# Attention computed for two batches in a row: TensorE's order in a fused graph layer with attention

## The chip, the cores and the metric

One core of a Trainium2 chip runs the whole kernel. The metric is the device time of one execution in microseconds (us), as the median of several executions. A single profiled execution gives the span that the views below are read from; in these runs it is 1.7 to 1.9 us shorter than the time.

Kernels are compared only within the same rounds. Ratios are computed as the mean time of one kernel's runs over that of the other's of the same rounds, so a ratio is not quite the ratio of the medians that I quote.

## The reference

Two layers over 128 batches of 128 nodes with 512 features, all in float32. Cut to what matters:

```python
# layer 0: conv with the adjacency matrix, maximum over features, residual, layer norm
A = einsum('od,bdn->bon', adj, x);  C = A + b          # W1 = W2 = adj
pre = A[:, :, None, :] + (C - A)[:, :, :, None]
x = layernorm(x + max(relu(pre), axis=-1))

# layer 1: masked attention with 8 heads of 64, projection, layer norm, residual, layer norm
q, k, v = split(x @ w_qkv)                              # 512 -> 3 * 512
attn = softmax(where(adj == 0, -inf, q @ k.T * 64 ** -0.5))
o = (attn @ v) @ w_proj + b_proj
x = layernorm(x + o + (layernorm(o) * gamma + beta))
```

## The kernel before

The 128 batches go through in 32 groups of four. TensorE does, per group, twelve products of 512 x 512 (eight for q and k over all four batches, four for v), four projections, and for every batch a convolution (`pa`), the transposes of x (`ptx`) and of the attention weights e (`ppt`), the scores (`psc`) and attention times v (`pav`).

Each product is done with split operands: an operand is cut into a high part and a low part, and a third form d corrects for what is lost. So a projection can start only when the output of attention has been split, which takes VectorE three operations and ScalarE one:

```python
def split(key, src, dsts):
    fh, fl, fd = dsts
    xh = work.tile([P, KC, P], FP, tag="xh", name=f"xh_{key}")
    nc.vector.tensor_scalar(xh.bitcast(I32), src.bitcast(I32), HIGH, None, op0=ALU.bitwise_and)
    hs[key] = fh, xh                                     # ScalarE casts xh into fh: split_high
    nc.vector.tensor_tensor(fl, src, xh, op=ALU.subtract)
    nc.vector.scalar_tensor_tensor(fd, fl.bitcast(FP), -HALF, xh, op0=ALU.mult, op1=ALU.add)

def product(key, two, terms):                            # terms: (stationary, moving) of h, l, d
    ...
    for kc in range(KC):
        h, l, _ = terms(kc)
        nc.tensor.matmul(pm, *h, start=(kc == 0), stop=False)
        nc.tensor.matmul(pm, *l, start=False, stop=(kc == KC - 1))
    for kc in range(KC):
        nc.tensor.matmul(pd, *terms(kc)[2], start=(kc == 0), stop=(kc == KC - 1))
```

The scores use 64 rows of the array, attention times v uses 64 columns, and everything else uses the full 128 x 128 (the trace writes the three as `64*128`, `128*64` and `128*128`):

```python
def scores(b):
    ...
        for s in range(2):
            hs = slice(s * HD, (s + 1) * HD)             # HD = 64
            nc.tensor.matmul(psc[:, s, hp, :], qkT[hs, hp, i, :], qkT[hs, KC + hp, i, :], ...)

def attend(b):
    ...
            nc.tensor.matmul(pavs[b][s * HD : (s + 1) * HD, hp, :],
                             v[:, h * HD : (h + 1) * HD], eT[:, s * HP + hp, :], ...)
```

The order is made by a plan. Every step is put down with a place in time, in planned microseconds; the list is sorted by place. On TensorE and ScalarE the sorted order is the order of the program; VectorE's order is chosen by a scheduler that takes the plan as its input. Before, the attention of a group is four blocks, one for each batch:

```python
for i in range(G):
    u = t + starts[i]
    last(0.0, transpose_e);  last(1.0, weights_T)        # batch of the group before
    now(0.95, scores);       now(2.1, masked);  now(3.5, row_max)
    nxt(2.0, transpose_x);   nxt(2.5, split_x)           # batch of the group after
    u += 2.5
    far(0.0, conv);          far(0.9, conv_max);  u += 0.9
    last(0.0, attend);       u += 1.0
    if i and 0 < g:
        projection((g - 1) * G + i - 1, u);  u += 2.8    # of the batch before
    last(0.1, heads)                                     # the split of attention's output
    ...                                                  # then a v product
```

## Time and profile before

| | before |
|---|---|
| time, median of 3 runs | 2081.63 us (2079.85 to 2081.64) |
| span of the profile | 2079.9 us |
| TensorE busy | 98% of the span |
| VectorE, ScalarE, GpSimd busy | 78%, 70%, 34% |
| first product of group 2 starts at | 144.02 us |
| from there to the first product of group 31 | 1837.96 us |
| from there to the end | 97.9 us |
| period of one group in the steady part | 63.467 us |

The lines are shown in the prediction. A line of a timeline gives the start, the duration, the engine, the source line, the operation, the tiles, the shapes and the count; matmuls overlap (in a product one is recorded as 0.40 us long and the next starts 0.23 us after it), so TensorE's time is read from start to start. A bracket at the end of a line is idle time of the engine before the instruction and what released it. "Period" in this document is always the time from the start of the first product of one group (the product (g, 4)) to that of the next.

### The profile page before, as it was taken

What the parts mean: (1) busy time and instruction counts of PE and PEld (TensorE: products, weight loads), DVE (VectorE), ACT (ScalarE), POOL (GpSimd) and SP (SyncE); (2) the same over time, 40 slices, a digit from 0 to 9 for tenths busy, and PEclk for the clock granted to TensorE, in tenths of its full rate; (3) what the DMA queues carried; (4) which work ended last, traced back from release to release, by engine and by line L of the source; (5) the groups of instructions that cost most, each with busy time, mean ns of one, the idle gap of its engine ahead of it and who ended that gap; (6) DMA issues with size and microseconds to landing.
All of it is one profiled execution on the core that took longest, in us unless ns stands there. A gap on an engine that the chain in (4) does not pass through costs nothing. (4 is left out here: it accounts for less than half of the span.)

```text
span 2079.9 us, 35025 instructions
## 1 busy us (share of the span) xinstructions
PE 2042.2 (98%) x12033; PEld 1591.0 (76%) x12033; DVE 1622.0 (78%) x2615; ACT 1451.7 (70%) x4130; POOL 701.5 (34%) x1329
## 2 busy tenths in 40 slices
PE   7899999999999999999999999999999999999997
PEld 5677777777777777777777777777777777777775
DVE  6787777887778877778877788777788777887787
ACT  5766767767767667677677676677776776766775
POOL 2123333323333233333233332333332333323434
PEclk8999999999999999999999999999999999999999
DMA  6345544455454455444554544554445545445533
GB/s 194 78 85 132 123 111 116 99 126 132 117 117 104 105 132 127 114 111 101 122 132 117 117 106 103 132 131 112 112 99 122 133 119 115 110 101 120 118 88 95
DMA packets 134434, 240.64 MB, mean 116 GB/s; under 512 B 14705, under 2 KB 18929, under 8 KB 134257
## 3 DMA queue, kind: packets, MB, share of 16 engines
q1 hardware_dynamic: 97680, 172.27, 27.1%
q0 software_dynamic: 36288, 66.08, 21.5%
q8 instruction: 95, 1.56, 0.3%
q14 instruction: 83, 0.67, 0.1%
q10 hardware_dynamic: 288, 0.07, 0.0%
HBM read 138.74 MB, written 100.66 MB: 115 GB/s over the span
## 5 line engine op out<-in xcount | busy, mean ns | idle before, releaser
L321 ACT ACTIVATE e<-e,nmax 128x128 f32<-128x128 f32 x1024 | 396.7, 391 | 6.3 <-DVE nmax L314 6.3
L380 POOL DMA_DIRECT2D xb<-o x124 | 120.2, 970 | 358.4 <-DVE o L385 342.1
L397 POOL TENSOR_SCALAR sum<-sum 128x1 f32<-128x1 f32 (+1 forms) x291 | 100.5, 345 | 391.5 <-ACT square L391 379.5
L213 POOL DMA_DIRECT2D x<-in_L_gnn_ln_beta_dram x128 | 115.6, 910 | 325.1 <-DMA x<-xt 308.3
L321 ACT ACTIVATION_READ_ACCUMULATOR e<-e,nmax 128x1 f32 x1024 | 194.1, 190 | 0.0
L398 POOL TENSOR_TENSOR sum<-sum,mhalf 128x1 f32<-128x1 f32 (+1 forms) x291 | 185.6, 638 | 22.5
L391 ACT ACTIVATE square<-o,sum 128x512 bf16<-128x512 f32 x256 | 183.2, 716 | 10.6 <-DVE o L385 8.7
L340 ACT COPY eT<-ppt 128x1024 f32<-128x1024 f32 x128 | 129.3, 1011 | 84.9 <-PE ppt L336 84.9
L349 PEld LDWEIGHTS pav<-eT,v 128*64 128x64 f32 x2048 | 109.2, 136 | 93.4 <-issue 47.4
L412 DVE SCALAR_TENSOR_TENSOR o<-o,sum,gamma_sb 128x512 f32<-128x512 f32 x128 | 96.1, 750 | 107.8 <-ACT square L391 104.8
L403 POOL TENSOR_SCALAR sum<-sum 128x1 f32<-128x1 f32 x256 | 157.5, 616 | 41.1 <-DVE o L385 35.6
L330 DVE TENSOR_TENSOR e<-e,sums 128x1024 f32<-128x1024 f32 x128 | 156.5, 1223 | 3.1
L306 DVE SCALAR_TENSOR_TENSOR e<-psc,mask 128x1024 f32<-128x1024 f32 x128 | 155.7, 1216 | 3.1 <-PE psc L299 3.0
L314 DVE TENSOR_REDUCE nmax<-e 128x8 f32<-128x1024 f32 x128 | 154.4, 1206 | 0.0
L299 PE MATMUL psc<-qkT 64*128 64x128 f32 x2048 | 149.9, 286 | 0.0
L299 PEld LDWEIGHTS psc<-qkT 64*128 64x128 f32 x2048 | 125.1, 188 | 24.1 <-issue 12.3
L349 PE MATMUL pav<-eT,v 128*64 128x128 f32 x2048 | 140.1, 279 | 2.1 <-ACT eT L340 2.1
L170 PE MATMUL pa<-xt,adjT 128*128 128x512 f32 x256 | 134.8, 612 | 2.7 <-DMA xt<-in_x_dram 2.3
L336 PE MATMUL ppt<-ident,e 128*128 128x128 f32 x1024 | 132.8, 273 | 0.0
L336 PEld LDWEIGHTS ppt<-ident,e 128*128 128x128 f32 x1024 | 119.5, 141 | 17.2 <-issue 0.5
L420 ACT ACTIVATE o<-o,sum 128x512 f32<-128x512 f32 x128 | 103.9, 811 | 33.5 <-POOL sum L406 33.4
L385 DVE SCALAR_TENSOR_TENSOR o<-o,sum,xb 128x512 f32<-128x512 f32 x128 | 95.7, 748 | 34.8 <-POOL sum L398 34.6
(4778 smaller groups left out, 5518.5 us busy)
## 6 DMA issues: line engine op xcount, KB each, us to landing
xt<-in_x_dram SPq DMA_DIRECT2D x128, 256.0 KB, 4.6
x<-xt SPq DMA_DIRECT2D x128, 256.0 KB, 3.3
x<-in_L_gnn_ln_beta_dram POOLq DMA_DIRECT2D x128, 256.0 KB, 6.4
xb<-x SPq DMA_DIRECT2D x128, 256.0 KB, 2.7
o<-in_L_gnn_b_proj_dram SPq DMA_DIRECT2D x128, 256.0 KB, 4.4
out_dram<-o SPq DMA_DIRECT2D x128, 256.0 KB, 2.3
xb<-o POOLq DMA_DIRECT2D x124, 256.0 KB, 3.5
wraw<-in_L_gnn_w_qkv_dram SPq DMA_DIRECT2D x12, 256.0 KB, 4.1
```

The costliest lines, as they stand in the source:

```text
L170: nc.tensor.matmul(pa[b], adjT, xs[b], start=True, stop=True)
L299: nc.tensor.matmul(psc[:, s, hp, :], qkT[hs, hp, i, :], qkT[hs, KC + hp, i, :], start=True, stop=True,)
L306: nc.vector.scalar_tensor_tensor(e, pscs.pop(b).rearrange("p s a m -> p (s a) m"), scale, mask_b, op0=ALU.mult, op1=ALU.add,)
L314: nc.vector.tensor_reduce(nmax, es[b], AX.X, ALU.max, negate=True)
L321: nc.scalar.activation(e[:, j, :], e[:, j, :], AF.Exp, bias=nmax[:, j : j + 1], accum_out=sums[:, j : j + 1],)
L330: nc.vector.tensor_tensor(e, e, sums[:, :, None].to_broadcast([P, H, P]), op=ALU.mult)
L336: nc.tensor.transpose(ppts[b][:, j, :], e[:, j, :], ident)
L340: nc.scalar.copy(eTs[b], ppts.pop(b))
L349: nc.tensor.matmul(pavs[b][s * HD : (s + 1) * HD, hp, :], v[:, h * HD : (h + 1) * HD], eT[:, s * HP + hp, :], start=True, stop=True,)
L391: nc.scalar.activation(square, x, AF.Square, bias=s[:, 0:1], scale=-float(D), accum_out=s[:, 1:2],)
L398: nc.gpsimd.tensor_tensor(s, s, mhalf[:, :n], op=ALU.pow)
L403: nc.gpsimd.tensor_scalar(s[:, 2:3], s[:, 0:1], -1.0 / D, None, op0=ALU.mult)
```

## The change

The intent is to run TensorE through one shape for two batches before it goes on to the next shape. The attention of a group becomes two pairs of batches, each with sixteen transposes of e, eight of x, two scores, two attention times v. The convolutions move into the dense phase. The first pair is followed by v products and projections in turn, the second pair by the convolutions and the q and k products. Buffers change with it: x 6 to 4, xb 3 to 2, eT 1 to 2, v 5 to 6.

```diff
-    xpool = ctx.enter_context(tc.tile_pool(name="xpool", bufs=6))
+    xpool = ctx.enter_context(tc.tile_pool(name="xpool", bufs=4))
@@ weights_T @@
-        eTs[b] = work.tile([P, H, P], FP, tag="eT", bufs=1, name=f"eT_{b}")
+        eTs[b] = work.tile([P, H, P], FP, tag="eT", bufs=2, name=f"eT_{b}")
@@ the plan: `attention` (above) and `beside_dense` are replaced @@
+    def attend_step(b, u, ready):
+        at(u, attend, b)
+        at(max(u + 1.0, ready), heads, b)
+        at(max(u + 1.0, ready) + 0.8, split_high, ("o", b))
+        return u + 1.0
+    def first_pair(g, t):
+        last, now, nxt = (g - 1) * G, g * G, (g + 1) * G
+        u = t
+        if g:
+            for i in range(2):
+                u = weights_step(last + i, u)
+        for i in range(2):
+            u = x_step(nxt + i, u)
+        for i in range(2):
+            at(u + 0.5, load_x, nxt + G + i) if g + 2 < NG else None
+        for i in range(2):
+            u = scores_step(now + i, u)
+        if g:
+            for i in range(2):
+                u = attend_step(last + i, u, u + 1.0 + 5.3 * i)
+        for i in range(2):
+            u = dense_step(g, 2 + i, u, i == 1)
+            if g:
+                u = project_step(last + i, u)
+        return u
+    def second_pair(g, t): ...        # the same for batches 2 and 3, without products
+    def dense_phase(g, t): ...        # convolutions, q and k products, two projections, two v products
```

(Cut: the places of the other steps, the order in which the weights are loaded at the start, and the last group. Also cut: which products take one tile of two PSUM banks and which take two single ones changes, and in the last two groups the split of o lies in the tiles of the q/k/v weights.)

## The prediction

> **What bounds the kernel now.** I read the page first, for the busy shares, then TensorE's timeline over one attention block in the middle of the run, then VectorE's timeline over the same microseconds, then the start of single TensorE instructions. The page (span, then engine: busy us, share, instructions):
>
> ```profile
> span 2079.9 us, 35025 instructions
> PE 2042.2 (98%) x12033; PEld 1591.0 (76%) x12033; DVE 1622.0 (78%) x2615; ACT 1451.7 (70%) x4130; POOL 701.5 (34%) x1329
> PEclk8999999999999999999999999999999999999999
> ```
>
> TensorE is the bound: busy for 98%, at a full granted clock after the start. The first product of group g (32 groups of four batches) starts every 63.467 us from group 2 to group 30, to the nanosecond; so almost nothing else is waited for, and the time is 29 equal periods plus a start and an end. The question is what stands inside a period. TensorE's timeline (start us, us, engine, line, operation, tiles, shapes, count):
>
> ```profile
> 1014.89 1.04 PE L336 MATMUL ppt<-ident,e 128*128 128x128 f32 x8
> 1015.86 1.16 PE L299 MATMUL psc<-qkT 64*128 64x128 f32 x16
> 1016.95 0.66 PE L220 MATMUL ptx<-ident,xt 128*128 128x128 f32 x4
> 1017.44 1.02 PE L170 MATMUL pa<-xt,adjT 128*128 128x512 f32 x2
> 1018.40 1.09 PE L349 MATMUL pav<-eT,v 128*64 128x128 f32 x16
> 1019.42 0.50 PE L253 MATMUL pp_('o', 57)_10000<-p_h,oh 128*128 128x512 f32 x1
> 1019.76 0.40 PE L254 MATMUL pp_('o', 57)_10000<-p_l,ol 128*128 128x512 f32 x1
> 1019.99 0.40 PE L253 MATMUL pp_('o', 57)_10000<-p_h,oh 128*128 128x512 f32 x1
> ```
>
> The reader is to see two things. The busy column overlaps, so only start to start counts: 0.97, 1.09, 0.49, 0.96, 1.02 us per batch. And there are three array shapes: scores use 64 rows (64\*128), attention times v uses 64 columns (128\*64), the rest 128\*128. The step after the last `pav` is 0.34 us instead of 0.23. Instruction by instruction, every change of shape shows the same bulge: the 16 `psc` matmuls start 7, 207, 7, 105, 7, 105 ... 7, 203 ns apart. From a change to the next instruction, steps over the undisturbed ones (109 for transposes, 105 and 103 between pairs, 432 for `pa`, 233 for products) are:
> - into scores: 203-109 = 94, then 207-105 = 102; out of scores: 203-105 = 98, then 165-109 = 56
> - into attend: 522-431 = 91, then 153-103 = 50; out of attend: 203-103 = 100, then 339-233 = 106
>
> Sum: 697 ns per batch, 2.79 us of each 63.47 us period.
>
> VectorE in the same block:
>
> ```profile
> 1018.06 1.22 DVE L306 SCALAR_TENSOR_TENSOR e<-psc,mask 128x1024 f32<-128x1024 f32 x1
> 1019.19 0.68 DVE L228 TENSOR_SCALAR xh<-ptx 128x512 int32<-128x512 int32 x1
> 1019.79 0.68 DVE L174 TENSOR_REDUCE rm<-pa 128x1 f32<-128x512 f32 x1
> 1020.38 0.68 DVE L230 TENSOR_TENSOR x_l<-ptx,xh 128x512 fp32r<-128x512 f32 x1
> 1020.98 1.21 DVE L314 TENSOR_REDUCE nmax<-e 128x8 f32<-128x1024 f32 x1
> 1022.11 0.68 DVE L231 SCALAR_TENSOR_TENSOR x_d<-x_l,xh 128x512 fp32r<-128x512 f32 x1
> ```
>
> No idle brackets: inside attention VectorE is full, one 512-wide operation each 0.60 us and one 1024-wide each 1.13 us (starts). It is second in line; its slack (78% overall) is in the dense phase.
>
> [...]
>
> **The change, part by part.** I compared the order of instructions of both built programs: each engine has the same operations, only order and buffers differ.
>
> (a) Fewer shape changes. TensorE now runs for two batches: 16 transposes of e, 8 of x, both scores, both attends, then a 128\*128 product or `pa`. Scores pass straight into attend. Per pair there remain: into scores 94+102, scores to attend 98+50 (estimate from the halves above; before has no clean steady example), out of attend 100+106 (100 where `pa` follows[...]). That is 550 and 444 ns, 0.99 us per group against 2.79: **-1.80 us per group**. All of it lies on TensorE, the bound. Over some 30 groups: -54 us, 2.6%, if nothing new waits.
>
> (b) A new short path. Before, a batch's projection came one attention block after its attend, about 7 us later. Now after the first pair come only one v product (2.9 us) and then that pair's first projection, which needs VectorE's split of `pav`. VectorE's order in the built program, every group alike, is: xh, xh, x_l, x_l, x_d, x_d (both x), mask, mask, xh of o, row maximum, o_l of o. I add starts, zero at the first e transpose. The first x transpose's last matmul starts at 16 x 109 + 327 = 2.07, ends 0.27 later, and VectorE takes 0.11 to start: 2.45. Then 6 x 0.60, 2 x 1.13, 0.60, 1.13: o_l starts at 10.03 and ends at 10.71. TensorE: 16 e and 8 x transposes 2.62, +0.09, scores 2 x 0.896 + 0.10, +0.10, attends 2 x 0.875 + 0.05, +0.10 = 6.60; v product 2.80 + 0.11: the projection would start at 9.50 and its second matmul, the first to read o_l, at 9.74. It can start at 10.71 + 0.06 (semaphore) + 0.20 (weight load) = 10.97. **+1.2 us per group**, in 30 groups: +37 us. The same sum for the other waits of the group finds none: the score buffer needs the copy of e's transpose (ScalarE, 3.0) by 3.7; the second pair has two `pa` and one q product before its projection (11.1 planned, o_l at 10.7); the buffer of the product after it frees at 13.8 against 13.9, near the edge.
>
> (c) Start and end. Before, the first q/k product of group 1 waited 4.1 us for x and then ran at a low clock:
>
> ```profile
> L253 PE MATMUL pp_(1, 4)_703<-x_h,w_h 128*128 128x512 f32 x4 | 2.7, 669 | 4.1 <-ACT x_h L240 4.1
> ```
>
> Now convolutions stand ahead of it: I expect 2 us of wait there and no slow clock, about -7 us. The first product needs all four x rather than one: +2. The end: before it loses 0.3 to 1.7 us at each of five waits for eT or oh; the new end has no v product to fill before the last projections, about 1.5 us twice: some -2. Estimates, sum -7.
>
> (d) Buffers (x loads 6 to 4, xb 3 to 2, eT 1 to 2, v 5 to 6): loads of x are issued after the transpose that frees the tile and have over 17 us to their convolution, against 4.6 us to landing. Hidden.
>
> Sum: 30 x (-1.80 + 1.23) = -17; -7 for start and end; less perhaps 3 already lost in small stalls of the old period (0.16 us). 2081.6 - 17 - 7 - 3 = about 2054. The projection's wait also swallows errors in (a) of the first pair, since VectorE then sets the time.
>
> **Rivals.**
> 1. All of (a) arrives, the projection does not wait: 2081.6 - 54 - 7 = 2020, 3% faster. For it: VectorE has 22% idle, the places look tuned to avoid this wait. Against: its order puts six splits, two masks and a row maximum first, at durations that hardly vary.
> 2. VectorE becomes the bound in attention: waits also at the second pair's projection and at the product buffer (margins 0.4 and 0.1 us). With 0.5 to 1 us more per group: 2070 to 2085, the same. For it: it is full in attention already. Against: pairs leave it 17 us for the first pair and the dense phase for the rest.
> 3. Scores to attend costs more than my halves. The single case at the end of before shows 281 ns against 203, though a copy was due there; +0.08 in the second pair only: +2 us.
> 4. A late x load, since two tiles fewer: 17 us of room speak against it.
>
> **Range and chances.** Centre 2052 (between the sum and a little of rival 1). The wait of 1.2 us could be 0.8 or 1.7 (12 us either way), start and end 7 us either way, other waits up to 10. So 2028 to 2072 in 8 of 10. Faster by over 2% means below 2040.0: 0.26. Slower by over 2%: 0.03.
>
> **What would show it.** Period between first products of groups: 62.9 us (61.7 under rival 1, 63.3 or more under rival 2). Scores and attend of two batches adjacent, steps near 200 ns at three places per pair. In the groups of lines, the projection's o_l matmuls idle about 1 us per group with VectorE `ol` (or ScalarE `oh`) as releaser; TensorE's busy time falls by the 54 us of (a) to near 1990. No such idle makes rival 1 right and my sum wrong; idle at q/k products released by VectorE or by masks is rival 2. I am wrong altogether if a change of shape costs the same however the shapes are ordered: then the period stays.

30 x (-1.80 + 1.23) = -17, then -7 for the start and the end and -3 for small stalls, take 2081.6 to about 2054. Some terms are estimates of mine:

- The 0.06 and 0.20 us in (b). In the trace of the kernel before, TensorE's first instruction starts 0.05 us after the end of the operation that it waited for (0.051 us after ScalarE's `x_h` at the product (1, 4)), and a weight load of a product takes 0.19 us (mean 188 ns). That the matmul can only start after both was assumed.
- The 0.11 us for VectorE's start in (b): in the same trace a `ptx` ends at 23.35 us and the `xh` that waits for it starts at 23.46.
- That the late operand holds up everything behind it on TensorE, so that the whole wait of (b) counts, was assumed; what the kernel after shows of it is under "Why the prediction was right", (b).
- That a wait of 2 us in (c) leaves the clock up was an expectation without a measurement. In the trace of the kernel before, a wait of 2.34 us ahead of a `pa` at 71.92 us is followed by a clock of 0.50 from 72.5 to 75.9 us.

## The result and the profile after

The changed kernel takes **2054.37 us** (median of 4 runs, 2052.57 to 2056.69), against 2081.15 us for the kernel before on the same chip (4 runs, 2079.85 to 2081.64). The ratio is 0.9873, 95% interval 0.9856 to 0.989: 1.3% faster, and so the same at the limit of 2%.

The page of the kernel after, its span, busy times and TensorE's granted clock:

```profile
span 2050.8 us, 35140 instructions
...
PE 1999.2 (97%) x12033; PEld 1599.6 (78%) x12033; DVE 1619.6 (79%) x2615; ACT 1449.4 (71%) x4130; POOL 712.7 (35%) x1484
...
PEclk8999999999999999999999999999999999999998
```

The number of instructions on TensorE, VectorE and ScalarE is the same. TensorE's busy time falls by 43.0 us, the span only by 29.1. The difference is idle time of TensorE that was not there before.

Where the 29.1 us of the two profiles come from:

| | before | after | difference |
|---|---|---|---|
| to the first product of group 2 | 144.02 | 131.73 | -12.3 |
| to the first product of group 31 (29 periods) | 1837.96 | 1816.97 | -21.0 |
| to the end | 97.9 | 102.07 | +4.2 |
| period | 63.467 | 62.673 | -0.794 |

Some of the first and last rows is work that only changed its side of the border: by the order of the two programs about 4.5 us of products and convolutions left the start and 2.8 us came to the end (my estimate from the 2.80 us of a product). The middle row is not 29 times the difference of the periods, because the last of the 29 is shorter than the others: 60.9 us before and 62.1 after.

TensorE's timeline in the kernel after, through the first pair of a group in the middle of the run. Only the first instructions of each block and the first two of the projection are shown:

```profile
1044.77 1.91 PE L339 MATMUL ppt<-ident,e 128*128 128x128 f32 x16
1046.52 1.04 PE L223 MATMUL ptx<-ident,xt 128*128 128x128 f32 x8
1047.48 2.06 PE L302 MATMUL psc<-qkT 64*128 64x128 f32 x32
1049.47 1.97 PE L352 MATMUL pav<-eT,v 128*64 128x128 f32 x32
1051.37 0.50 PE L256 MATMUL pm_(16, 2)_10574<-w_h,x_h 128*128 128x512 f32 x1
...
1054.41 0.50 PE L256 MATMUL pp_('o', 60)_10595<-p_h,oh 128*128 128x512 f32 x1
1055.48 0.50 PE L257 MATMUL pp_('o', 60)_10595<-p_l,ol 128*128 128x512 f32 x1 [0.58 <-DVE ol L233]
```

The pairs are there: 16, 8, 32 and 32 matmuls in one row each. The last line is the new wait. From the first matmul of the projection to the second it is 1.07 us; in a projection without a wait that step is 0.235 us. The releaser is VectorE's `ol`, the low part of attention's output. (The bracket gives only the idle part, 0.58 us, because the matmul before it counts as busy for 0.50 us, though the next one normally starts 0.235 us after it.)

VectorE's timeline over the same microseconds shows what stands ahead of `ol`:

```profile
1047.15 1.29 DVE L231 TENSOR_SCALAR xh<-ptx 128x512 int32<-128x512 int32 x2 [1.43 <-PE ptx L223]
1048.36 1.28 DVE L233 TENSOR_TENSOR x_l<-ptx,xh 128x512 fp32r<-128x512 f32 x2
1049.56 1.28 DVE L234 SCALAR_TENSOR_TENSOR x_d<-x_l,xh 128x512 fp32r<-128x512 f32 x2
1050.76 2.35 DVE L309 SCALAR_TENSOR_TENSOR e<-psc,mask 128x1024 f32<-128x1024 f32 x2
1053.02 0.68 DVE L231 TENSOR_SCALAR xh_('o', 60)_10557<-pav 128x512 int32<-128x512 int32 x1
1053.62 1.21 DVE L317 TENSOR_REDUCE nmax<-e 128x8 f32<-128x1024 f32 x1
1054.75 0.68 DVE L233 TENSOR_TENSOR ol<-pav,xh_('o', 60)_10557 128x512 fp32r<-128x512 f32 x1
```

Six splits of x, two masks, one split of o and a row maximum without a gap, then `ol`. Its input `pav` was ready long before: the first batch's attention ends at about 1050.6, by the start of the block, 0.875 us for one batch and 0.27 us for its last matmul. `ol` ends at 1055.43, and TensorE goes on 0.05 us later.

The waits of the kernel after (out, source line, releaser: total us, times, longest us) have this line once for every group:

```profile
PE pp_('o', 48)_8687 L257 <- DVE ol L233: 0.6, 1, 0.6
```

### The profile page after: what moved, and what is told of

Its sections match the earlier page's. It is cut to its first block, busy times and chain, and to the rows that moved or that the text cites. A ratio compares the mean times of both kernels' runs of the same rounds, so it can differ in the third digit from the quotient of the medians.

```text
span 2050.8 us, 35140 instructions
## 1 busy us (share of the span) xinstructions
PE 1999.2 (97%) x12033; PEld 1599.6 (78%) x12033; DVE 1619.6 (79%) x2615; ACT 1449.4 (71%) x4130; POOL 712.7 (35%) x1484
## 4 chain that ended last, share of the span: by engine, by line
PE 82%; DVE 13%; issue 2%; ACT 1%; DMA 1%; POOL 1%; SPq 0%; POOLq 0%; DVEq 0%; ACTq 0%
PE pa L173 6%; PE ppt L339 5%; DVE e L309 4%; PE psc L302 3%; PE pav L352 3%; DVE xh L231 2%; DVE x_l L233 2%; PE ptx L223 2%; DVE x_d L234 2%; DVE ol L233 1%; DMA xb<-o 1%; ACT e L324 0%; DVE nmax L317 0%; POOL sum L409 0%; ACT square L402 0%
## 5 line engine op out<-in xcount | busy, mean ns | idle before, releaser
L409 POOL TENSOR_TENSOR sum<-sum,mhalf 128x1 f32<-128x1 f32 (+1 forms) x322 | 204.5, 635 | 26.7
L391 POOL DMA_DIRECT2D xb<-o x124 | 113.2, 913 | 225.9 <-DVE sums L332 107.3
L183 POOL TENSOR_SCALAR rm<-rm,b_sb 128x2 f32<-128x2 f32 (+1 forms) x66 | 66.7, 1011 | 284.8 <-DVE rm L177 259.5
L343 ACT COPY eT<-ppt 128x1024 f32<-128x1024 f32 x128 | 123.4, 1015 | 35.0 <-PE ppt L339 35.0
L414 POOL TENSOR_SCALAR sum<-sum 128x1 f32<-128x1 f32 x256 | 99.7, 392 | 122.4 <-DVE o L396 122.2
L408 POOL TENSOR_SCALAR sum<-sum 128x1 f32<-128x1 f32 (+1 forms) x322 | 64.4, 200 | 201.3 <-ACT square L402 186.2
L302 PE MATMUL psc<-qkT 64*128 64x128 f32 x2048 | 131.9, 278 | 0.8 <-ACT eT L343 0.7
L352 PE MATMUL pav<-eT,v 128*64 128x128 f32 x2048 | 127.5, 278 | 2.8 <-ACT eT L343 2.8
L173 PE MATMUL pa<-xt,adjT 128*128 128x512 f32 x256 | 126.2, 617 | 0.4 <-DVE adjT L102 0.4
L339 PE MATMUL ppt<-ident,e 128*128 128x128 f32 x1024 | 122.4, 272 | 0.6 <-DVE v L291 0.6
```

Of the source, the lines that this page charges most:

```text
L173: nc.tensor.matmul(pa[b], adjT, xs[b], start=True, stop=True)
L339: nc.tensor.transpose(ppts[b][:, j, :], e[:, j, :], ident)
L343: nc.scalar.copy(eTs[b], ppts.pop(b))
L352: nc.tensor.matmul(pavs[b][s * HD : (s + 1) * HD, hp, :], v[:, h * HD : (h + 1) * HD], eT[:, s * HP + hp, :], start=True, stop=True,)
L391: nc.gpsimd.dma_start(xbs[b], os[b], accum_op=ALU.add)
L409: nc.gpsimd.tensor_tensor(s, s, mhalf[:, :n], op=ALU.pow)
```

## The experiments

I had one theory and several rivals. **Theory:** the period is what TensorE needs without waits, 61.62 us in the new order by my sum (the measured 62.673 less 1.09 gives 61.58), plus the wait at the first projection, 1.09 us, and that wait is set by the order of operations on VectorE. **Rivals:** the shape changes saved less than I counted; the wait has another cause (ScalarE's `oh`, the smaller number of x buffers); or the wait is a symptom and comes back elsewhere when it is taken away. Twelve more kernels ran, and all give correct results. Three of them, x_late, beta_later and attend_first_late_beta, turned out not to be experiments: in their traces the order of instructions on all five engines is the same as in the kernel that they were to change, so they are repeats of it.

| run | median us (range) | ratio to before | 95% interval | period us |
|---|---|---|---|---|
| after | 2054.37 (2052.57 to 2056.69) | 0.9873 | 0.9856 to 0.989 | 62.673 |
| adjacent_before | 2059.29 (2059.05 to 2059.5) | 0.9898 | 0.9883 to 0.9913 | 62.713 |
| split_second_pair | 2063.93 (2062.04 to 2068.17) | 0.9927 | 0.991 to 0.9943 | 63.03 |
| split_first_pair | 2035.02 (2031.64 to 2035.96) | 0.9778 | 0.9763 to 0.9793 | 61.966 |
| v_first | 2048.63 (2047.93 to 2050.47) | 0.9848 | 0.9833 to 0.9863 | 62.573 |
| v_first_ready | 2044.65 (2042.42 to 2046.02) | 0.9826 | 0.9811 to 0.9841 | 62.30 |
| rowmax_after_ol | 2051.86 (2048.2 to 2053.8) | 0.986 | 0.9845 to 0.9875 | 62.24 and 62.68 |
| proj_early | 2215.32 (2214.62 to 2218.42) | 1.0651 | 1.0633 to 1.0669 | 67.8 to 68.6, once 66.2 |
| x_late | 2053.35 (2051.66 to 2056.34) | 0.9871 | 0.9856 to 0.9886 | 62.68 |
| attend_first | 2030.11 (2027.88 to 2031.03) | 0.9746 | 0.9732 to 0.9761 | 61.833 |
| attend_first_both | 2027.81 (2026.35 to 2032.06) | 0.9742 | 0.9726 to 0.9759 | 61.77 |
| attend_first_late_beta | 2027.64 (2026.15 to 2031.63) | 0.9739 | 0.9725 to 0.9754 | 61.833 |
| beta_later | 2054.95 (2052.68 to 2057.17) | 0.9867 | 0.9853 to 0.9882 | 62.667 |

The kernel before took 2080.64 to 2082.59 us (medians of 7 runs) on the chips of these runs. The repeats show how far a median of four can be off without any change: 2053.35 to 2054.95 us for the kernel after (on different chips), 2027.64 and 2030.11 us for attend_first (on one chip).

### Does the shape change cost what I counted? Undoing the pairing, one pair at a time

split_second_pair lets each batch of the second pair go through scores and attention alone, as scores, attend, scores, attend. The second pair has no wait on VectorE, so only the shape changes should tell.

```diff
         for i in range(2, 4):
             u = scores_step(now + i, u)
-        if g:
-            for i in range(2, 4):
-                u = attend_step(last + i, u, u + 1.0 + (0.0, 7.1 if g + 2 < NG else 5.3)[i - 2])
+            if g:
+                u = attend_step(last + i, u, u + (2.0, 8.1 if g + 2 < NG else 6.3)[i - 2])
```

> The same edit in the second pair of each group only, where no projection waits. Theory: each of two added shape changes costs what the single ones cost before (into attend 98+50, back into scores 100+102 ns): 0.35 us per group, period 63.02, about 2065 us. Rival (the gain of pairing comes from hidden semaphore waits, not from shapes): no difference, 2054.

Measured: the period is 63.03 us, +0.35, and the time 2063.93 us. Scores and attention of the second pair take 4.232 us from start to start instead of 3.882. Each extra switch between scores and attention costs real time, and the size is what I had counted.

split_first_pair does the same in the first pair, the one that waits.

```diff
         for i in range(2):
             u = scores_step(now + i, u)
-        if g:
-            for i in range(2):
-                u = attend_step(last + i, u, u + 1.0 + 5.3 * i)
+            if g:
+                u = attend_step(last + i, u, u + (2.0, 6.3)[i])
```

> The changed kernel, but in the first pair of each group scores, attend, scores, attend in place of both scores, both attends: one change of array shape into attend and one back into scores more per pair. My theory (TensorE is the bound except where the first projection waits for o_l, and VectorE's order sets that wait): the built program now has VectorE's second mask after o's xh, so o_l ends at 9.6 us instead of 10.7 after the pair's start; the added shape changes cost 0.35 us, the wait of 1.09 us goes; period 62.67 - 1.09 + 0.35 = 61.95, about 2033 us. Rival (fewer shape changes is all that matters): slower by 0.35 x 30 = 10 us, about 2065.

Measured: 2035.02 us, 2.2% below the kernel before and faster than the changed kernel, although TensorE has *more* shape changes. The period is 61.966 us. VectorE's timeline of this run shows why (the operations ahead of `ol` after the x splits):

```profile
1040.37 1.22 DVE L309 SCALAR_TENSOR_TENSOR e<-psc,mask 128x1024 f32<-128x1024 f32 x1
1041.51 0.68 DVE L231 TENSOR_SCALAR xh_('o', 60)_10555<-pav 128x512 int32<-128x512 int32 x1
1042.10 1.22 DVE L309 SCALAR_TENSOR_TENSOR e<-psc,mask 128x1024 f32<-128x1024 f32 x1
1043.23 0.68 DVE L233 TENSOR_TENSOR ol<-pav,xh_('o', 60)_10555 128x512 fp32r<-128x512 f32 x1
```

The row maximum is now behind `ol`, and TensorE arrives 0.35 us later. The first transpose of e in this group starts at 1034.39, so `ol` starts at 8.84 us from there instead of 9.98. The projection takes 2.80 us: no wait at all. The balance closes: -1.09 for the wait, +0.35 for the shapes, sum -0.74; measured -0.71.

These two runs together are the size of both terms of the prediction in isolation: a split of a pair costs 0.35 us where nothing waits, and gives 1.09 us back where VectorE was late.

### Is it VectorE's order? The row maximum behind `ol`

```diff
-            at(t + (8.7, 13.5, 29.5, 34.0)[i], row_max, g * G + i)
-            at(t + (10.3, 15.5, 30.5, 36.0)[i], exps, g * G + i)
+            at(t + (12.0, 13.5, 29.5, 34.0)[i], row_max, g * G + i)
+            at(t + (12.1, 15.5, 30.5, 36.0)[i], exps, g * G + i)
```

> The changed kernel with one row maximum (first batch of the first pair) placed after o_l on VectorE; TensorE's order is untouched. o's second xh takes its place before o_l, so o_l comes 1.13 - 0.60 = 0.53 us earlier. Theory: the wait at the first projection falls by 0.53 us to about 0.5 us, period 62.14, about 2038 us. Rival (TensorE's own order or the ScalarE cast oh sets the wait): no difference, 2054.

Measured: 2051.86 us, a miss. The edit did not do what I meant. In the built program the row maximum stands behind `ol` only in groups 2 to 16; in group 1 and from group 17 on the scheduler has put it ahead, although the planned places are the same in every group. In the first groups the period is 62.24 us, in the later ones 62.68. So half of the run is the experiment and half the control: 0.43 us per group where the order changed (I had said 0.53), nothing where it did not. The wait for `ol` itself did fall by 0.53: from the first matmul of the projection to the second it is 0.54 us instead of 1.07. But `od`, which now stands behind the row maximum, comes late and costs one step 0.10 us more (0.331 instead of 0.235). So the projection in the changed groups takes 3.295 us instead of 3.749. It still waits for `ol`, because the second batch's `xh` now stands ahead of it. The reason why the scheduler's order turns in the middle is not known to me.

### Does a product in between hide it? Both v products first

v_first runs both v products ahead of both projections, so that the first projection comes 2.8 us later, and the second keeps its place.

```diff
         for i in range(2):
             u = dense_step(g, 2 + i, u, i == 1)
+        for i in range(2):
             if g:
                 u = project_step(last + i, u)
```

> Only the order on TensorE changed: both v products ahead of both projections. In the built program VectorE then has the weights of the first batch (which wait for ScalarE's exponentials) and the last v sum ahead of o_l of the second batch. Theory: no wait at the first projection, but 0.8 us at the second one, for o_l; period about 62.4, about 2046 us. Rival (room on TensorE is all that counts): period 61.6, 2023.

Measured: 2048.63 us, period 62.573. The first projection takes 2.80 us, without a wait. The second projection takes 3.782 us, and the waits name the same operation of the other batch:

```profile
PE pm_('o', 17)_3654 L257 <- DVE ol L233: 0.7, 1, 0.7
```

The wait moved by one batch and lost only a tenth of a microsecond (0.98 us in place of 1.09). VectorE splits the pair's two outputs one after the other, and in this order the second split is the one that comes late.

v_first_ready also asks for the second split earlier, and puts off the multiplication by the softmax sums.

```diff
-                u = attend_step(last + i, u, u + 1.0 + 5.3 * i)
+                u = attend_step(last + i, u, u + 1.0 + 3.5 * i)
@@ and v_first, and @@
-            at(t + (24.0, 30.0, 42.0, 46.0)[i], weights, g * G + i)
+            at(t + (31.0, 32.0, 42.0, 46.0)[i], weights, g * G + i)
```

> The changed kernel with both v products of the first pair ahead of both projections on TensorE, and o's split of the second batch and the weights placed so that VectorE has o_l in time. The first projection gets 2.8 us more room. Theory: no wait for o_l of the first batch, about 0.2 us for the second, period 61.6 to 61.9, about 2026 us, 2.7% under the kernel before. Rival (VectorE is the bound in attention as a whole): the wait moves on, period stays above 62.4, 2045 or more.

Measured: 2044.65 us and a period of 62.30; I had expected 61.6 to 61.9. The wait at the second projection shrinks to 0.39 us, but the projection behind the product (g+1, 5) in the dense phase now waits for ScalarE's `oh`: from the start of that product to its own start it is 3.026 us instead of 2.799, and it takes 2.907 us instead of 2.802. That what was put off on VectorE delays this `oh` is my reading; no run tests it alone. The pieces sum to 0.72 us: about two thirds of the wait of 1.09 us came back elsewhere, as that rival says, and a third was gained (62.673 to 62.30).

### The attention of the last group ahead of the scores

The split of o needs `pav` only; nothing forces the scores ahead of it. attend_first swaps the two steps in the first pair. TensorE keeps its three shape changes per pair.

```diff
-        for i in range(2):
-            u = scores_step(now + i, u)
         if g:
             for i in range(2):
-                u = attend_step(last + i, u, u + 1.0 + 5.3 * i)
+                u = attend_step(last + i, u, u + (2.6, 6.3)[i])
+        for i in range(2):
+            u = scores_step(now + i, u)
```

> In the first pair both attention-times-v steps stand ahead of both scores steps; the second pair and all else as in the changed kernel. The number of shape changes per pair stays (550 ns). In the built program VectorE's order is then xh, xh, x_l, x_l, x_d, x_d, xh of o, mask, o_l of o, mask, o_d, row maximum, in every group. My theory (the order on VectorE ahead of o_l sets the wait at the first projection): by the starts of the timeline o_l begins 7.77 us after the first transpose of e and ends at 8.45, ahead of the 9.74 at which its first matmul stands; no wait there, a period of 61.62 us and a time of 2020 to 2027 us. Rival (the wait has a cause on TensorE or ScalarE, for instance oh, which the projection reads first): a wait of about 1 us stays and the time is 2050.

Measured: 2030.11 us (2027.88 to 2031.03), ratio 0.9746, so 2.5% faster than the kernel before. TensorE's timeline of attend_first in the same group:

```profile
1035.43 1.91 PE L339 MATMUL ppt<-ident,e 128*128 128x128 f32 x16
...
1038.14 1.97 PE L352 MATMUL pav<-eT,v 128*64 128x128 f32 x32
1040.04 2.06 PE L302 MATMUL psc<-qkT 64*128 64x128 f32 x32
...
1045.15 0.40 PE L257 MATMUL pp_('o', 60)_10595<-p_l,ol 128*128 128x512 f32 x1
```

and VectorE's:

```profile
1041.42 0.68 DVE L231 TENSOR_SCALAR xh_('o', 60)_10553<-pav 128x512 int32<-128x512 int32 x1
1042.02 1.22 DVE L309 SCALAR_TENSOR_TENSOR e<-psc,mask 128x1024 f32<-128x1024 f32 x1
1043.15 0.68 DVE L233 TENSOR_TENSOR ol<-pav,xh_('o', 60)_10553 128x512 fp32r<-128x512 f32 x1
1043.75 1.22 DVE L309 SCALAR_TENSOR_TENSOR e<-psc,mask 128x1024 f32<-128x1024 f32 x1
```

`ol` starts 7.72 us after the first transpose of e (I had summed 7.77), ends at 8.40, and its first matmul starts at 9.72 with no bracket. The wait is gone, without a single extra shape change, by moving one row ahead of another. This is the most direct evidence for the theory: the same operations and the same number of shape changes, with `pav` before `psc` on TensorE, the splits of o placed to match, and `ol` earlier on VectorE. It also speaks against the smaller number of x buffers as a cause, since they stay at four here.

The time misses my range of 2020 to 2027 by 3 us. The period is 61.833 us and not 61.62. The second projection takes 2.864 us instead of 2.80. The product (g+1, 5) in the dense phase starts 0.07 us late and takes 0.11 us longer; its weight load names the releaser, VectorE adding the second half of the q/k product before, which must free a product's buffer:

```profile
1067.45 0.19 PEld L256 LDWEIGHTS pp_(17, 5)_10855<-x_h,w_h 128*128 128x128 f32 x1 [0.34 <-DVE qkT L291]
```

In 30 groups the 0.21 us are 6 us, which is what the median is above the middle of my range. So the rival that the wait comes back elsewhere is true for a fifth of it.

attend_first_both does the same in both pairs.

```diff
@@ attend_first, and in second_pair @@
-        for i in range(2, 4):
-            u = scores_step(now + i, u)
         if g:
             for i in range(2, 4):
-                u = attend_step(last + i, u, u + 1.0 + (0.0, 7.1 if g + 2 < NG else 5.3)[i - 2])
+                u = attend_step(last + i, u, u + (2.6, 8.1 if g + 2 < NG else 6.3)[i - 2])
+        for i in range(2, 4):
+            u = scores_step(now + i, u)
```

> Attention times v ahead of scores in both pairs. The second pair had no wait in the changed kernel, so by my theory its order gains nothing: period 61.62 us and the same time as attend_first within 3 us. Rival (VectorE's order in the second pair also costs, through later buffers of products): a period under 61.5 and a time over 3 us below attend_first; or, if the masks that now come later delay the exponentials, a longer period by 0.1 to 0.5 us (3 to 15 us more).

Measured: 2027.81 us, period 61.77. The order of the second pair is worth 0.06 us per group at most; the difference of 2.3 us to attend_first is inside the spread of both.

### The projection sooner: what a longer wait costs

proj_early runs each projection ahead of the v product, so that TensorE stands with nothing to do. I meant to see the wait of 1.09 us grow by the 2.8 us of the product.

```diff
         for i in range(2):
-            u = dense_step(g, 2 + i, u, i == 1)
             if g:
                 u = project_step(last + i, u)
+            u = dense_step(g, 2 + i, u, i == 1)
@@ and attend_step as in v_first_ready @@
```

> The opposite: each projection ahead of its v product, so that the first projection has no product before it. VectorE's o_l still ends 10.7 us after the pair's start. Theory: the wait at the first projection grows by the product that stood before it, 2.8 us per group, period 65.4 to 65.5, about 2137 us. Rival (TensorE would reach it late anyway): within 10 us of 2054.

Measured: 2215.32 us, 6.5% slower, against the 2137 I expected. The wait came as foreseen. In group 16 the first matmul of the projection starts 9.635 us after the first transpose of e, and in the kernel after at 9.636: VectorE's split, through ScalarE's `oh` that follows it, sets this time, whatever TensorE does meanwhile. But the group grows by 5.1 to 5.9 us instead of 2.8, in all groups from 2 on but one. TensorE's timeline in another group:

```profile
1060.80 1.97 PE L352 MATMUL pav<-eT,v 128*64 128x128 f32 x32
1065.74 0.79 PE L256 MATMUL pp_('o', 56)_9938<-p_h,oh 128*128 128x512 f32 x1 [2.97 <-ACT oh L243]
...
1067.83 0.63 PE L257 MATMUL pp_('o', 56)_9938<-p_l,ol 128*128 128x512 f32 x1
1068.25 0.63 PE L256 MATMUL pp_('o', 56)_9938<-p_h,oh 128*128 128x512 f32 x1
```

From 1067.83 to 1068.25 is one step of 0.43 us; undisturbed it is 0.233. The table of stretches (stretch, us, busy us and count of TensorE, weight loads, VectorE, ScalarE, GpSimd, then the granted clock, DMA share and GB/s) shows the clock:

```profile
1062.80:1065.70 2.90, 0.00 (x0) 0.00 (x0) 2.90 (x4) 0.62 (x1) 0.00 (x0) 0.91 0.57 217
1068.00:1070.00 2.00, 2.00 (x7) 1.52 (x6) 1.08 (x1) 1.57 (x9) 0.00 (x0) 0.50 0.98 125
1072.00:1074.00 2.00, 2.00 (x10) 1.58 (x9) 1.97 (x6) 0.11 (x1) 0.00 (x0) 1.00 0.29 39
```

After 2.97 us of idleness TensorE runs at half its clock until about 1072.0. From the mean of 0.77 in the stretch 1065.00 to 1065.30, the clock fell at about 1065.16, so 2.4 us after the end of the last matmul, and stayed low for 6.8 us (both are my working). In group 16 this adds 2.18 us to the projection: 4.857 us from its second matmul to its end, against 2.677 in the kernel after. Another 0.76 us are a wait of the next transposes of e; its releaser is VectorE's addition into v, the last reader of a product's buffer. With the 2.80 us of the product the balance of group 16 closes: 5.74, measured 5.75.

One group shows the same idle time without the slow clock. The bracket before the projection is 2.97 us in each of the 30 groups. In group 6 the clock stays at 1.00 all the same, the projection takes 3.74 us as in the kernel after, and the period is 66.23 us: 3.56 more, which is the 2.80 that I expected and the 0.76. In the other 29 the clock records of the trace put the fall 2.1 to 5.3 us after the end of the last matmul, so in part of them only when TensorE was busy again, and the slow stretch lasts 3.41 or 6.83 us.

So 2.97 us of idle time were followed by half the clock (0.50) in 29 groups of 30, and once they were not. The wait of the kernel after, 1.09 us in two pieces, leaves the clock at 1.00 in the stretch from 1054.0 to 1058.0. So the new wait of the change costs its length and no more. The wait of proj_early, 1.09 and 2.80 us, costs 1.5 to 2.4 us more than in group 6 wherever the clock falls from group 2 on. At which length this begins, these runs do not show: near the end of the kernel after one wait of 2.41 us is followed by half the clock (0.50 from 2017.8 to 2021.2 us), and in group 6 one of 2.97 us is not.

### Shapes without the new order

adjacent_before edits the kernel before: scores go next to attention within each batch, one batch at a time, with transposes of x and the convolution ahead of them.

```diff
-            now(0.95, scores);  now(2.1, masked)
+            now(2.35, scores);  now(3.4, masked)
-            nxt(2.0, transpose_x);  nxt(2.5, split_x)
+            nxt(0.9, transpose_x);  nxt(1.4, split_x)
-                far(0.0, conv);   far(0.9, conv_max)
+                far(-1.1, conv);  far(-0.1, conv_max)
```

(Two statements are written on one line here; the program has them on two.)

> The kernel before, without pairs: only x's transposes and the convolution moved ahead of the scores, so that scores and attend stand side by side. Per batch one change of shape fewer. Theory: steps saved are out of scores 98+56 and into attend 91+50, less scores to attend 98+50, so 0.15 us per batch, 0.6 per group, period 62.9, about 2062 us. Rival: the scores come 1.4 us later and VectorE, full in attention, passes the delay on: no gain or a loss.

Measured: 2059.29 us, period 62.713, -0.754. The shape changes account for 0.59 us of it (147 ns per batch). The other 0.16 us are stalls of the old period, and the starts of single instructions show where they are. In the second block of each group of the kernel before (groups 8, 15 and 20 were looked at) the first `pa` starts 173 ns after the last transpose of x instead of 109, and the second 533 ns after the first instead of 432: 165 ns. The trace's releasers are ScalarE's copy of a v product and VectorE's `ol`, each the last reader of a tile in the PSUM pool (`ps_1`) from which `pa` takes its own; that these tiles are the ones which `pa` then gets is inferred. In adjacent_before these steps are 109 and 432 in all four blocks. So an edit of six numbers in the kernel before gives 1.0%, most of what the whole change gives, because it takes a third of its shape gain and none of its wait.

### Buffers, and the start

x_late was to put the loads of x 8 us later, to see whether four x buffers in place of six are close to a wait.

```diff
-            at(u + 0.5, load_x, nxt + G + i) if g + 2 < NG else None
+            at(u + 8.5, load_x, nxt + G + i) if g + 2 < NG else None
```

(in both pairs)

> The changed kernel with the loads of x issued 8 us later, to test that the smaller x pool costs nothing. Theory: hidden, the time stays within 3 us of 2054. Rival: x loads stand on the path through layer 0, slower by up to 8 us per group.

Measured: 2053.35 us, period 62.68, no wait on x. But the edit moved nothing. In group 16 the four loads are issued 38.05, 38.49, 57.04 and 57.48 us after the first product of the group in the kernel after, and 38.07, 38.50, 57.03 and 57.47 us in x_late; from group 1 on no load differs by more than 0.11 us. A planned place is the order of the program on TensorE and ScalarE only; the DMA queues are arranged by the scheduler, and here it kept its order. So this run says nothing on the buffers. The trace of the kernel after does: from group 2 on every load lands at least 12 us before the convolution that reads it, and no wait for one is named.

The start of the kernel was left. All runs that derive from the kernel after spread over 2.5 to 6 us, the kernel before over 1.5 to 5, and adjacent_before over 0.5. In the profiles the product (1, 4) starts anywhere from 72.9 to 79.9 us, and where it starts late, the product (0, 0) has waited for its weights and then run at a low clock (in beta_later, where (1, 4) starts at 78.0 us, (0, 0) waits 0.22 and 1.90 us for `w_h`, and the first matmuls of the next product, at 60.28 and 60.71, are 0.43 us apart instead of 0.23). Four accumulating transfers of beta are issued at about the same time as the loads of these weights, so I suspected them. beta_later was to move them away in the kernel after, attend_first_late_beta on top of attend_first.

```diff
-        at(30.0 + b, beta_0, b)
+        at(66.0 + b, beta_0, b)
```

> The changed kernel with only the four beta_0 transfers of the first group moved 36 us later. Theory on the start: period stays 62.67, first product of group 1 at 74.5 us or earlier, 2050 to 2052 us with a spread under 2 us. Rival: no difference to the changed kernel (2052.6 to 2056.7).

> As attend_first, and the four accumulating transfers of beta_0 of the first group are placed 36 us later in the plan, away from the weight loads at the start. Theory on the start (these transfers slow the weight loads at about 33 us in some runs, so that the very first product waits for w_h and then runs at a low clock): first product of group 1 at 74.5 us or earlier, no wait of product (0,0) on w_h, time about 2 us below attend_first and a narrower spread (2018 to 2024). Rival (the spread at the start has another cause, for instance how the transfers fall from run to run): the same time as attend_first and the same spread of some 4 us.

Measured: beta_later takes 2054.95 us, with a spread of 4.5 us, as the kernel after. Its waits still have the line

```profile
PE pp_(0, 0)_490 L256 <- ACT w_h L146: 2.1, 2, 1.9
```

and (1, 4) starts at 78.0 us. attend_first_late_beta had no such wait in its profile and (1, 4) at 72.9 us, but its median and its spread (2026.15 to 2031.63) are those of its neighbours. Neither run tests the suspicion, because the transfers did not move: the four are issued at 16.5, 20.4, 28.0 and 30.2 us in the kernel after, at 16.5, 23.3, 26.9 and 32.8 us in beta_later, and at 16.2, 23.3, 26.4 and 33.3 us in attend_first_late_beta. Whether they delay the weights stays open. What the runs do show is that the same order of instructions gives both kinds of start. The slowest load of weights doesn't decide it: it took 7.5 us to land in attend_first, which had the wait, and 7.5 us in attend_first_late_beta, which had none. Why the start changes from run to run stays open.

## Why the prediction was right

I predicted 2052 us, with 2028 to 2072 as the range, and 0.71 for "within 2%". Measured: 2054.37 us, 1.3% faster. The worked sum in the text said about 2054. By its steps:

**(a) Fewer shape changes, -1.80 us per group: right, with one term too small.** The steps around the shape changes in the kernel after are those of the list: from scores to attention 98 and 50 ns, which I had put together from halves. Rival 3 (281 ns in place of 203) does not hold: the step is 203. The one miss is the way out of attention into `pa`. I had counted 100 ns at the change and nothing at the step after it; the trace shows 202 ns and then 533 instead of 428, so 105 ns more, once per group. TensorE's busy time fell to 1999.2 us and not to the 1990 I named: about half of each new wait lies inside matmuls that count as busy (1.09 us of wait against 0.58 us of idle bracket). split_second_pair shows the size of a change of shape alone: 0.35 us for two more switches into scores and out again.

**(b) The new wait, +1.23 us per group: right in kind, 0.14 too large.** `ol` starts 9.98 us after the first transpose of e, where I had 10.03; it ends at 10.66 (10.71), and its first matmul starts at 10.71 (10.97). The step that was mis-sized is the last: I had added 0.06 us for the release and 0.20 for the weight load, estimates near the 0.05 and 0.19 us in the trace of the kernel before, one after the other. The trace of the kernel after shows 0.05 us to the recorded start of the matmul and a longer step after it (0.338 us in place of 0.231), so 0.16 together. Besides, the first matmul of the projection waits 0.14 us for `oh`, which I had not counted. The sum of the pieces, 0.14 + 0.84 + 0.11, is the 1.09 us that split_first_pair and attend_first then took away. The late operand held up what is behind it, as I had assumed: the next product, (16, 3), starts at 1058.16 us, 0.23 us after the last matmul of the projection has started.

These terms give -1.80 + 0.105 + 1.09 = -0.61 per group. The stalls of the old period, for which I had named 0.16 us, are the 0.165 us at `pa` found above; with them the sum is -0.77, against the measured -0.794. Over 30 groups the miss in (a) is +3 us and that in (b) -4 us. That the total came within 1 us of the sum is partly luck: they cancel, and the start alone varies by more than that.

**(c) Start and end, -7 us: right in the sum, by parts not well founded.** The two borders moved -12.3 and +4.2 us. Without the work that only changed sides they moved by about -7.8 and +1.4, -6.4 together, where I had -5 and -2. The slow clock of the first q/k product of group 1 is gone as predicted: before, its wait is 4.1 us and the clock is 0.50 from 79.3 to 86.1 us; after, its wait is 0.5 us and the clock is 1.00 from 70.0 to 84.0. The end went the other way. The view of the waits still names 2.4 us for eT at one `pav`, and 1.3 and 1.2 us at two of the last projections. From the end of the first of these (2.41 us, until 2018.06) the clock is at 0.50, by its records from 2017.8 to 2021.2 us, and the `pav` of that pair take 3.42 us from start to start instead of 1.90. So this wait costs 1.5 us more than its length, as much as the end grew; the prediction counted no slow clock there. And the start varies by several us between runs, which I had not seen coming; a single profile cannot settle a term of 7 us.

**(d) Buffers: right.** The trace of the kernel after has no wait for a load of x, and at least 12 us between landing and use from group 2 on; I had over 17 us from issue to use, 4.6 of them to landing. x_late adds nothing to this. One sentence above (a) is wrong: the engines do not all have the same operations, GpSimd has 155 instructions more. It is busy for 35% of the span, and no wait of TensorE between groups 2 and 30 names it.

Of the rivals, number 1 (no wait at the projection, 2020 us) describes what the change could have been: attend_first is this kernel, and it is at 2030. Number 2 (VectorE as the bound) is not in the kernel after: there is no wait at the second pair and none at the product buffers. It shows up only when the first wait is gone: the 0.21 us of attend_first are at the product buffers, for which the prediction had a margin of 0.1 us.

## What to carry to other kernels

When a change reorders the bounding engine, write down for each operand on the new short path the full list of operations that the *other* engine has ahead of it, with start-to-start durations; here that sum was right to 0.05 us and decided that most of a 54 us saving would not arrive. Then ask whether the consumer's input can be produced first: moving attention times v ahead of the scores took the wait away without giving up a single shape change, where delaying the consumer (v_first) only moved it. Order on an engine that a scheduler arranges must be checked in the built program for every iteration: one of my edits held for half of them, and three moved nothing at all. A run whose time does not change is evidence only when its trace shows that the edit took hold.

## What these traces show of TensorE

- What a change of array shape costs. In the kernel after, in the middle of the run, the steps at a change exceed the undisturbed ones by 94 + 102 ns into the scores (203 and 207 ns, undisturbed 109 and 105), by 98 + 50 from the scores into attention (202 and 154, undisturbed about 104), and by 100 and then 105 or 106 out of attention into the full array (202, then 338 in a product, undisturbed 232; 202, then 533 at `pa`, undisturbed 428). The sums are 0.15 to 0.21 us per change. Two additional switches per pair cost 0.35 us in split_second_pair.
- Which waits were followed by half the clock: 2.97 us in 29 of 30 groups of proj_early (0.50), 2.41 us near the end of the kernel after (0.50 from 2017.8 to 2021.2 us), and 1.78 us at the start of v_first, where the steps of the product (0, 1) are 0.43 us until 59.33 us and 0.23 from 59.60 on. Others were not: 2.97 us in group 6 of proj_early (1.00), and 1.64 us at the start of split_first_pair, where the steps of the product (0, 1) are 0.23 us. The slow stretches of proj_early last 3.41 or 6.83 us.
- What a late operand adds to a stream of matmuls. In group 16 of the kernel after, the recorded start of the matmul that reads `ol` follows the end of VectorE's operation by 0.05 us, and the next step is 0.338 us, 0.107 longer than the undisturbed 0.231.
